# A two-layer block on one core: norm weights folded into a projection, one activation table set through attention, and gate steps moved into the expert stage

## The chip, the cores and the metric

The kernel runs on one core of a Trainium2 chip. The metric is the time of one execution in device microseconds (us). All data are float32. The core's engines are called as the profile calls them: PE is the matrix engine (PEld its weight loads), DVE the vector engine, ACT the scalar engine with its tables of functions, POOL the general engine, SP the engine whose queue issues most DMAs.

## The reference, cut to what matters

The input `x` is 4 rows (b = 0..3) of 512 tokens by 512 channels, `fside` has the same shape. Two layers follow each other; each part adds its result to `x`.

```python
def gate(r, k, v, w, u, time_emb):      # the four "cond" parts, l = 0..3; k = v = fside
    decay = f(w, time_emb)
    ek, ekv = exp(min(k, 30)), exp(min(k, 30)) * v
    # running sums over the tokens, forwards (nf, df) and backwards (nb, db): a = a * decay + e
    num = nf + nb - ekv + euk * v;  den = df + db - ek + euk     # euk = exp(min(u + k, 30))
    return sigmoid(r) * (num / max(den, 1e-8)) * (0.8 + 0.2 * tf)

x = x + mamba2(gate0(x))       # projection, short convolution, silu, a scan over the tokens in tiles;
                               # y = y * silu(z); y = y * rsqrt(mean(y*y) + eps) * norm_w; y @ out_proj_w.T
x = x + experts(gate1(x))      # top 2 of 8 experts per token, each a gated 512-512 network
x = x + attention(gate2(x))    # 16 heads in 4 groups with a shared key and value, causal softmax
x = x + ffn(gate3(x))          # silu(x @ gate) * (x @ up) @ down, 1408 wide
```

Everything of a gate but `sigmoid(r)` depends on `fside` alone, so it can be made before the row of `x` that it is for is ready.

## The kernel before

The program is unrolled, and written for a framework in which the code states instructions and tiles. A scheduler then orders the instructions of each engine by their place in the code, their data and the buffers of the tile pools, and sets the semaphores. `with after(engine)` holds a step behind the last instruction that the code has stated for that engine. Buffers with the same tag share `bufs` slots, so a tile waits until an older one is released. PSUM has three tags: `mm` (4 slots), `tp` (2 slots, `ps_tp`) and `acc` (2 slots).

Four stages follow each other:

- **Scan stage** (layer 0, `mamba2`; 16 tiles of 128 tokens, 4 per row). `start_tile` makes `z`, `start_scores`, `decays` and `outputs` make the tile's `y`. One half tile later, for the tile before it (`old`), `squares` and `norm` make the factor of the root mean square, `turn` transposes `y` into `pyt` (PSUM, tag `tp`) and writes it to `yT` times `norm_w` (first half: one DVE multiply, L1219; second half: four ACT multiplies, L1227), `project` multiplies it with `wot` (L1235), `scale` and `add_x` finish. `time_steps` and `sums` run once per row: `sums` (from L973) makes running sums over the tile's tokens with three products into `ppr` (tag `tp`), copies them to `cs` on DVE (L991), transposes `cs` on PE (`pcs`, L993), copies that to `csT` (L995) and stores it; `load_sums` reads it back, spread over the partitions.
- In the same stage the **gates** are made. `gate_pair` makes half a gate (2 of the 4 blocks of 128 channels): loads (`kt` L237, `ek` L244, `ekv` L246), four forward scans (L256) and four backward ones (L262) on DVE, sums (L273, L275, L277), then on ACT `Relu` (L313), `Ln` and `Exp` for the reciprocal, three more DVE steps (L319, L323, L328), and a store of `g` (L330). It is a generator: `pump(n)` runs n stretches of it, `nudge()` one short step. `gated` loads a made gate and applies it: four `Tanh` on ACT and four DVE steps (L383).
- `choose_experts` and `route` pick the experts of a row's tokens. They are a generator too (`routing`), stepped at fixed places of the tile loop.
- **Expert stage.** The tokens are sorted into 39 blocks of 128, one expert per block. `moe.round()` runs one block: first half (`pg` L775, `pn` L786), `finish` of the block before, `down` (`po` L808) of the block two before. Weights (`w1` in two halves of 1 MB, `w2` 1 MB) go out on SP's queue when a block's expert differs from the one that its buffer holds. The first 17 blocks use one set of buffers, the others two in turn. After each round but the last few, `more` runs `pump()` for the gates of layers l = 2 and 3.
- **Attention.** 16 groups of 4 heads, four (one per row) for each of the four key groups. Per head: `queries` (L1565), `scores` (psc L1582, mask L1585, maximum L1587, `Exp` on ACT L1592, L1594), then for the head before it `context` (L1605, L1608, L1614). After four heads `dense` (L1629). In each of a head's four score blocks `nudge()` runs a step of a gate. In the first groups `combine(b + 1)` adds the experts' results to the next row, and `gated(2, b + 1, ...)` gives that row's attention input; if its gate is not made yet, `gated` makes it there.
- **Feed-forward.** L1691, L1696, L1706 with `Silu` (L1700).

ACT holds one set of function tables at a time. `Tables` (the object `act`) loads a set by name (L112) and keeps the activations called through `act(...)` behind that load; the set stays until the next `act.use`. The set LOG_EXP has `Exp` and `Ln`, EXP has `Exp` and `Tanh`, SILU has `Silu` and `Tanh`. From `act.leave()` on (the last part of the scan stage's code) it keeps no record, and the compiler puts a load before every activation whose function is not in the set at hand.

Of the kernel before, what the change touches and what calls it, by code (L numbers as in the profile page):

```python
# [10 lines left out]
F32 = mybir.dt.float32  # L11
# [6 lines left out]
P = 128  # L18
# [62 lines left out]
def block_kernel(ctx: ExitStack, tc: tile.TileContext, a: dict, out: bass.AP):  # L81
# [424 lines left out]

    def route(lg, b, fine):
        n = NT * E
# [56 lines left out]
        yield  # L565
        pt = ps_tp("ptok")
        over = lambda v: v.unsqueeze(2).to_broadcast([P, NT, P])
        lanes = lane.unsqueeze(1).to_broadcast([P, NT, P])
        for c, (q, s_) in enumerate(vq):
            ov = tmp.tile([P, NT, P], F32, tag="th", name="ov")  # L570
            nc.vector.tensor_tensor(ov, lanes, over(q), ALU.is_equal)
            nc.vector.tensor_tensor(ov, ov, over(res_id[c][:, bt_]), ALU.mult)
            os_ = tmp.tile([P, NT, P], F32, tag="th", name="os")
            nc.vector.tensor_tensor(os_, lanes, over(s_), ALU.is_equal)
            for t in range(NT):
                nc.tensor.matmul(
                    pt[:, :P], lhsT=ov[:, t, :], rhs=os_[:, t, :],
                    start=(t == 0 and c == 0), stop=(t == NT - 1 and c == 1),
                )
# [15 lines left out]
    def choose_experts(b, xb, parts, pool, fine=False, **kw):  # L595

        lg = rt.tile([P, NT, E], F32, tag="lg", name="lg", bufs=2)
        nt = NT // parts
        for i in range(parts):
            h = gated(1, b, xb, pool, slice(i * nt * P, (i + 1) * nt * P), **kw)  # L600
            if fine:
                yield
            logits(h, b, lg, i * nt, nt)
            yield
        yield from route(lg, b, fine)

# [254 lines left out]
    with ExitStack() as ph:  # L861
# [64 lines left out]
        nc.sync.dma_start(out=wot, in_=a["out_projT"].rearrange("(k p) m -> p k m", p=P))  # L926

        def time_steps(w):

# [43 lines left out]
        def sums(w):  # L973
# [14 lines left out]
            nc.vector.tensor_tensor(dte, dt, ex[:, 1], ALU.mult)  # L988

            cs = sm.tile([P, n], F32, tag="cs", name="cs", bufs=2)  # L990
            nc.vector.tensor_copy(cs, pp[:, :n])  # L991
            pcs = ps_tp("pcs")
            nc.tensor.transpose(pcs[:n, :P], cs, ident)  # L993
            csT = four[:n, 0:2, :].rearrange("p i t -> p (i t)")
            nc.vector.tensor_copy(csT, pcs[:n, :P])  # L995
            nc.sync.dma_start(out=cs_d[w.b], in_=csT)
# [213 lines left out]
        def turn(u):  # L1210

            u.yT = sm.tile([P, NDI, P], F32, tag="yT", name="yT")
            for hh in range(2):
                pyt = ps_tp("pyt")
                for j in range(4):
                    js = slice(j * P, (j + 1) * P)
                    nc.tensor.transpose(pyt[:, js], u.y[hh][:, js], ident)
                if hh == 0:
                    nc.vector.tensor_tensor(  # L1219
                        u.yT[:, :4, :],  # L1220
                        pyt.rearrange("p (j t) -> p j t", t=P),
                        col("norm_w", 0, 4).unsqueeze(2).to_broadcast([P, 4, P]),
                        ALU.mult,
                    )
                else:
                    for j in range(4):
                        nc.scalar.mul(  # L1227
                            u.yT[:, 4 + j, :], pyt[:, j * P : (j + 1) * P], col("norm_w", 4 + j)
                        )

# [67 lines left out]
        for b in range(B):  # L1298
# [6 lines left out]
            for t in range(NT):  # L1305
# [86 lines left out]
                with after(*ENGINES):  # L1392
                    next(routing, None)
                    if b == B - 1 and t == 1:
                        next(routing)
# [75 lines left out]
    with tc.tile_pool(name="moe_w2", bufs=1, reuse_waits="tile") as wm:  # L1471
# [4 lines left out]
        def more(limit):  # L1476
            while moe.i < min(limit, moe.known):
                moe.round()
                if moe.i < NBLK - NT:
                    with after(nc.vector):  # L1480
                        pump()

# [28 lines left out]
    with att as ph:  # L1511
# [64 lines left out]
        def scores(u, i, qT):  # L1576

            prs = []
            for qi in range(NT):
# [11 lines left out]
                rsum = sm.tile([P, 1], F32, tag="rsum", name="rsum", bufs=4)  # L1591
                nc.scalar.activation(pr, psc[:, :n], AF.Exp, bias=nmax, accum_out=rsum)  # L1592
                nc.vector.reciprocal(rsum, rsum)
# [50 lines left out]
        def begin(n):  # L1644
# [5 lines left out]
            return groups[g, b], queries(groups[g, b], i)  # L1650

        groups = {}
        ready, held = begin(0), None
        for n, (g, b, i) in enumerate(heads_):
            u, qT = ready
            if g == 0 and i == 1 and b + 1 < B:
                combine(b + 1)
                hs[b + 1] = gated(2, b + 1, x[b + 1], gp, tag="h", name=f"h2_{b + 1}")
            if n + 1 < len(heads_):
                ready = begin(n + 1)  # L1660
            prs = scores(u, i, qT)
            if held is not None:
# [7 lines left out]
        for _ in making:  # L1670
            pass


    with ExitStack() as ph:
# [9 lines left out]
        for b in range(B):  # L1684
            h = gated(3, b, x[b], gp, tag="h", name=f"h3_{b}")
            hd = []
            for i in range(NFF):
# [11 lines left out]
                hi = sm.tile([P, T], F32, tag="hd", name="hd", bufs=NFF + 2)  # L1699
                nc.scalar.activation(hi, pg, AF.Silu, scale=col("gate_s", i))  # L1700
                nc.vector.scalar_tensor_tensor(hi, pu, col("up_s", i), hi, ALU.mult, ALU.mult)  # L1701
# [85 lines left out]
```

## Time and profile before

| | us |
|---|---|
| median of 3 runs (lowest, highest) | 2587.08 (2586.99, 2592.27) |
| the profiled execution | 2591.44 |
| its span in the trace | 2589.7 |
| PE busy in it | 2446.0 (94%) |
| DVE, ACT, POOL busy | 1409.8, 1032.3, 250.4 |

The profiled execution is 4.36 us longer than the median of the runs, and 1.74 us of it lie around the span. A row of the profile names a line of the code, an engine, an operation and the tiles (out<-in), then count, busy time in us and the mean of one in ns, and last the idle time of the engine ahead of it with the instruction that ended it. PEclk is the granted share of PE's clock.

By their chain of work the stages lie at about 0 to 665 us (scan, with a start of 80 us), 665 to 1165 us (experts), 1165 to 2128 us (attention) and 2128 to 2590 us (feed-forward).

### The profile page before, as it was taken

The numbers are of one execution on the slowest core, as the hardware profiler recorded it, in microseconds if no ns is written. First come the engines' busy times: TensorE is split into PE (matmuls) and PEld (weight loads), VectorE is DVE, ScalarE is ACT, GpSimd is POOL, SyncE is SP. The second block draws the span as 40 slices with busy tenths as digits, with TensorE's granted clock in tenths as the row PEclk, the third lists the DMA queues.
The fourth block names the chain that finished last, engine by engine and source line by source line (L and its number), as shares of the span: only waits on it lengthen the run. The fifth ranks groups of instructions, "written<-read, shape, count | busy, mean of one in ns | idle before, by whom it ended". The sixth has DMA issues, their size and how long they took to land.

```text
span 2589.7 us, 24584 instructions
## 1 busy us (share of the span) xinstructions
PE 2446.0 (94%) x8204; PEld 1301.0 (50%) x8204; DVE 1409.8 (54%) x2786; ACT 1032.3 (40%) x2129; POOL 250.4 (10%) x301
## 2 busy tenths in 40 slices
PE   3889998999999999999989999999999999999999
PEld 1555555556544444445545555555555554444444
DVE  8789998997335555646686554556544441010010
ACT  4666756657222333325554444344443431000000
POOL 1031323313211111120000000000000000000000
PEclk9979998999899999999999999999999999999999
DMA  6222523324244697745231101110000012000000
GB/s 217 77 94 76 188 69 112 131 80 159 66 175 140 223 337 283 274 177 163 75 92 46 46 27 29 45 45 30 21 25 17 17 69 82 17 0 16 8 8 16
DMA packets 88510, 244.09 MB, mean 94 GB/s; under 512 B 9536, under 2 KB 19136, under 8 KB 79296
## 3 DMA queue, kind: packets, MB, share of 16 engines
q1 hardware_dynamic: 79200, 215.78, 24.3%
q0 software_dynamic: 6880, 22.55, 2.5%
q10 hardware_dynamic: 2304, 4.20, 0.4%
q8 instruction: 65, 1.06, 0.2%
q14 instruction: 61, 0.50, 0.1%
HBM read 284.82 MB, written 47.05 MB: 128 GB/s over the span
## 4 chain that ended last, share of the span: by engine, by line
PE 75%; DVE 16%; ACT 4%; DMA 3%; issue 1%; POOL 0%; SPq 0%; ACTq 0%; DVEq 0%
PE pd L1629 8%; PE pq L1565 7%; PE pfu L1696 6%; PE pfo L1706 6%; PE pfg L1691 6%; PE pctx L1614 5%; PE po L808 5%; PE pg L775 5%; PE pn L786 5%; PE psc L1582 3%; PE pc L1007 2%; PE po L1235 2%; PE pv L1551 2%; PE ptp L1605 2%; PE pz L1078 2%; PE pk L1543 2%
## 5 line engine op out<-in xcount | busy, mean ns | idle before, releaser
L1565 PE MATMUL pq<-h,wq 128*128 128x512 f32 x512 | 248.0, 600 | 10.9 <-ACT pr L1592 10.9
L1629 PE MATMUL pd<-cx,wd 128*128 128x512 f32 x512 | 222.9, 593 | 1.3 <-DVE xr L1637 1.3
L1007 PE MATMUL pc<-h,wxb 128*128 128x512 f32 x320 | 151.6, 629 | 46.1 <-DVE h L1275 39.0
L1700 ACT ACTIVATE hd<-pfg,cols 128x512 f32<-128x512 f32 x44 | 30.3, 688 | 380.8 <-PE pfg L1691 380.8
L1701 DVE SCALAR_TENSOR_TENSOR hd<-pfu,cols,hd 128x512 f32<-128x512 f32 x44 | 33.0, 751 | 269.1 <-PE pfu L1696 269.0
L1585 DVE TENSOR_TENSOR psc<-psc,mask 128x128 f32<-128x128 f32 x256 | 72.2, 288 | 192.9 <-PE psc L1582 192.9
L1592 ACT ACTIVATE pr<-psc,nmax 128x128 f32<-128x128 f32 (+3 forms) x256 | 135.5, 530 | 95.6 <-DVE nmax L1587 94.9
L1614 PE MATMUL pctx<-pT,v 128*128 128x512 f32 (+3 forms) x512 | 153.6, 443 | 8.5 <-ACT pT L1608 5.1
L1696 PE MATMUL pfu<-h,ffu 128*128 128x512 f32 x352 | 158.7, 592 | 0.8 <-DMA ffu<-in_upT 0.8
L1691 PE MATMUL pfg<-h,ffg 128*128 128x512 f32 x352 | 158.6, 592 | 0.0
L1582 PE MATMUL psc<-kT,qT 128*128 128x128 f32 (+3 forms) x512 | 153.1, 439 | 3.1 <-ACT qT L1573 1.6
L1629 PEld LDWEIGHTS pd<-cx,wd 128*128 128x128 f32 x512 | 95.9, 190 | 116.8 <-issue 110.0
L1706 PE MATMUL pfo<-hd,ffd 128*128 128x512 f32 x352 | 151.7, 592 | 0.0
L775 PE MATMUL pg<-w,hT 128*128 128x512 f32 x312 | 144.7, 606 | 4.3 <-DMA w<-in_w1x 4.3
L1614 PEld LDWEIGHTS pctx<-pT,v 128*128 128x128 f32 x512 | 93.4, 190 | 99.6 <-issue 35.9
L808 PE MATMUL po<-w,yT 128*128 128x512 f32 x312 | 142.3, 596 | 1.2 <-DMA w<-in_w2x 1.2
L786 PE MATMUL pn<-w,hT 128*128 128x512 f32 x312 | 140.7, 592 | 0.0
L1637 DVE TENSOR_TENSOR xr<-xr,pd 128x512 f32<-128x512 f32 x64 | 44.0, 687 | 169.3 <-PE pd L1629 169.3
L1587 DVE TENSOR_REDUCE nmax<-psc 128x1 f32<-128x128 f32 (+3 forms) x256 | 124.0, 486 | 2.6
L1007 PEld LDWEIGHTS pc<-h,wxb 128*128 128x128 f32 x320 | 62.6, 201 | 119.6 <-issue 73.8
L1565 PEld LDWEIGHTS pq<-h,wq 128*128 128x128 f32 x512 | 87.1, 192 | 69.4 <-issue 56.1
L1605 PEld LDWEIGHTS ptp<-ident,pr 128*128 128x128 f32 x640 | 77.8, 142 | 87.4 <-issue 38.4
(308 smaller groups left out, 4220.2 us busy)
## 6 DMA issues: line engine op xcount, KB each, us to landing
w<-in_w1x SPq DMA_DIRECT2D x80, 1024.0 KB
w<-in_w2x SPq DMA_DIRECT2D x40, 1024.0 KB
wb<-in_b1x SPq DMA_DIRECT2D x40, 512.0 KB
lm<-cs SPq DMA_DIRECT2D x32, 512.0 KB
kt<-in_fT SPq DMA_DIRECT2D x62, 256.0 KB
ek<-ek SPq DMA_DIRECT2D x62, 256.0 KB
ekv<-ekv SPq DMA_DIRECT2D x62, 256.0 KB
g<-num SPq DMA_DIRECT2D x30, 512.0 KB
```

The lines of the kernel that those rows point to most:

```text
L775: nc.tensor.matmul(pg, lhsT=hT[:, k, :], rhs=self.w1[s][0][:, k, :], start=(k == 0), stop=(k == NC - 1))
L786: nc.tensor.matmul(pn, lhsT=hT[:, k, :], rhs=self.w1[s][1][:, k, :], start=(k == 0), stop=(k == NC - 1))
L808: nc.tensor.matmul(po, lhsT=yT[:, j, :], rhs=self.w2[s][:, j, :], start=(j == 0), stop=(j == NI - 1))
L1007: nc.tensor.matmul(pc, lhsT=wxb[:, k, m * P : (m + 1) * P], rhs=h[:, k, :], start=(k == 0), stop=(k == NC - 1),)
L1565: nc.tensor.matmul(pq, lhsT=u.wq[:, k, i * KVC : (i + 1) * KVC], rhs=u.h[:, k, :], start=(k == 0), stop=(k == NC - 1),)
L1582: nc.tensor.matmul(psc[:, :n], lhsT=qT[:, qi * P : n], rhs=u.kT[:, :n], start=True, stop=True)
L1592: nc.scalar.activation(pr, psc[:, :n], AF.Exp, bias=nmax, accum_out=rsum)
L1614: nc.tensor.matmul(pctx[:, kj * P :], lhsT=u.v[:, kj, :], rhs=pT[:, kj, kj * P :], start=(kj == 0), stop=(kj == NT - 1),)
L1629: nc.tensor.matmul(po, lhsT=u.wd[:, i, m * P : (m + 1) * P], rhs=u.ctxT[i], start=(i == 0), stop=(i == HPG - 1),)
L1691: nc.tensor.matmul(pg, lhsT=wg[:, k, cs], rhs=h[:, k, :], start=(k == 0), stop=(k == NC - 1))
L1696: nc.tensor.matmul(pu, lhsT=wu[:, k, cs], rhs=h[:, k, :], start=(k == 0), stop=(k == NC - 1))
L1706: nc.tensor.matmul(po, lhsT=wdn[:, i, m * P : (m + 1) * P], rhs=hd[i], start=(i == 0), stop=(i == NFF - 1),)
```

## The change

Five edits:

1. `norm_w` is multiplied into the rows of `wot` once, by 8 POOL instructions of 128x512, after its load. `turn` then only copies: two ACT copies of 128x512 per tile, and nothing on DVE.
2. In `sums` the transpose of `cs` is replaced by a fourth product into `ppr` that gives the turned sums at once (`dA` as the stationary side, `tri_le` moving); `pcs` is gone. `cs` is still copied.
3. In `route` for rows 0 to 2, the first pair of comparisons takes its own tile instead of the two `th` slots, a further `yield` stands after it, and the PSUM tile `ptok` is taken after the comparisons instead of ahead of them. In the last row `routing` is stepped once more.
4. In the expert stage `pump()` becomes `pump(1 + moe.i % 2)`: three stretches in two rounds.
5. In attention and feed-forward all activations go through `act`: LOG_EXP is held, EXP is loaded for each of three `gated` calls, and LOG_EXP again behind it; SILU is loaded at attention's end. `gated(2, b + 1, ...)` moves from the group's second head to its third, behind `begin(n + 1)`.

```diff
@@ route
+            if fine and c == 0:
+                both = pool.tile([P, 2, NT, P], F32, **kw)
+                ov, os_ = both[:, 0], both[:, 1]
+            else:
+                ov = tmp.tile([P, NT, P], F32, tag="th", name="ov")
+                os_ = tmp.tile([P, NT, P], F32, tag="th", name="os")
...
+            if fine and c == 0:
+                yield
+            if pt is None:
+                pt = ps_tp("ptok")
@@ scan stage, after the load of wot
+        for k in range(NDI):
+            nc.gpsimd.tensor_scalar(wot[:, k, :], wot[:, k, :], col("norm_w", k), None, ALU.mult)
@@ sums
+            nc.tensor.matmul(
+                pp[:n, 3 * n : 3 * n + P], lhsT=dA.rearrange("p t h -> p (t h)"), rhs=tri_le,
+                start=True, stop=True,
+            )
             cs = sm.tile([P, n], F32, tag="cs", name="cs", bufs=2)
             nc.vector.tensor_copy(cs, pp[:, :n])
-            pcs = ps_tp("pcs")
-            nc.tensor.transpose(pcs[:n, :P], cs, ident)
             csT = four[:n, 0:2, :].rearrange("p i t -> p (i t)")
-            nc.vector.tensor_copy(csT, pcs[:n, :P])
+            nc.vector.tensor_copy(csT, pp[:n, 3 * n : 3 * n + P])
@@ turn
-                if hh == 0:
-                    nc.vector.tensor_tensor(u.yT[:, :4, :], ...
-                else:
-                    for j in range(4):
-                        nc.scalar.mul(u.yT[:, 4 + j, :], ...
+                nc.scalar.copy(
+                    u.yT[:, hh * 4 : (hh + 1) * 4, :].rearrange("p j t -> p (j t)"), pyt
+                )
@@ tile loop
-                    if b == B - 1 and t == 1:
+                    if b == B - 1 and t < 2:
                         next(routing)
@@ more
-                        pump()
+                        pump(1 + moe.i % 2)
@@ scores
-                nc.scalar.activation(pr, psc[:, :n], AF.Exp, bias=nmax, accum_out=rsum)
+                act(pr, psc[:, :n], AF.Exp, bias=nmax, accum_out=rsum)
@@ attention's loop
+        with after(nc.scalar):
+            act.use(act.LOG_EXP)
...
             if g == 0 and i == 1 and b + 1 < B:
                 combine(b + 1)
-                hs[b + 1] = gated(2, b + 1, x[b + 1], gp, tag="h", name=f"h2_{b + 1}")
             if n + 1 < len(heads_):
                 ready = begin(n + 1)
+            if g == 0 and i == 2 and b + 1 < B:
+                act.use(act.EXP)
+                hs[b + 1] = gated(2, b + 1, x[b + 1], gp, tag="h", name=f"h2_{b + 1}")
+                act.use(act.LOG_EXP)
...
+        act.use(act.SILU)
@@ feed-forward
-                nc.scalar.activation(hi, pg, AF.Silu, scale=col("gate_s", i))
+                act(hi, pg, AF.Silu, scale=col("gate_s", i))
```

More of the change, by code (lines that the diff above doesn't have):

```diff
@@ L505, in logits, with route @@
             nc.sync.dma_start(out=rows_h[lo : lo + P, :], in_=hr)
-    def route(lg, b, fine):
+    def route(lg, b, fine, pool, **kw):
         n = NT * E
@@ L565, in route @@
         yield
-        pt = ps_tp("ptok")
         over = lambda v: v.unsqueeze(2).to_broadcast([P, NT, P])
         lanes = lane.unsqueeze(1).to_broadcast([P, NT, P])
+        pt = None
         for c, (q, s_) in enumerate(vq):
-            ov = tmp.tile([P, NT, P], F32, tag="th", name="ov")
+            if fine and c == 0:
[4 more added lines that the diff above has]
+                os_ = tmp.tile([P, NT, P], F32, tag="th", name="os")
             nc.vector.tensor_tensor(ov, lanes, over(q), ALU.is_equal)
             nc.vector.tensor_tensor(ov, ov, over(res_id[c][:, bt_]), ALU.mult)
-            os_ = tmp.tile([P, NT, P], F32, tag="th", name="os")
             nc.vector.tensor_tensor(os_, lanes, over(s_), ALU.is_equal)
+            if fine and c == 0:
+                yield
+            if pt is None:
+                pt = ps_tp("ptok")
             for t in range(NT):
@@ L604, in choose_experts @@
             yield
-        yield from route(lg, b, fine)
+        yield from route(lg, b, fine, pool, **kw)
     taken = rt.tile([P, 1], F32, name="taken")
@@ L1217, in turn @@
                     nc.tensor.transpose(pyt[:, js], u.y[hh][:, js], ident)
-                if hh == 0:
[L1219 to L1224, printed above, removed]
-                else:
-                    for j in range(4):
-                        nc.scalar.mul(
-                            u.yT[:, 4 + j, :], pyt[:, j * P : (j + 1) * P], col("norm_w", 4 + j)
-                        )
+                nc.scalar.copy(
+                    u.yT[:, hh * 4 : (hh + 1) * 4, :].rearrange("p j t -> p (j t)"), pyt
+                )
         def project(u):
```

## The prediction

> **What bounds the kernel now.** I read the page's slices first, then the engines' busy time by stage, who waited for whom on PE, and last single waits in the timeline.
>
> ```profile
> PE   3889998999999999999989999999999999999999
> DVE  8789998997335555646686554556544441010010
> ```
>
> PE is the bound nearly everywhere; DVE is about as full as PE in the scan stage (first ten slices) and half empty behind it. By stage (PE, PEld, DVE, ACT, POOL busy, granted clock, DMA share, GB/s):
>
> ```profile
> 80.00:665.00 585.00, 543.73 (x2249) 328.58 (x2249) 501.28 (x854) 386.57 (x766) 145.72 (x164) 0.94 0.33 109
> 665.00:1165.00 500.00, 482.50 (x1432) 239.06 (x1432) 249.30 (x402) 135.39 (x221) 94.68 (x107) 0.97 0.60 217
> 1165.00:1340.00 175.00, 157.84 (x578) 87.25 (x577) 125.73 (x276) 93.04 (x199) 1.11 (x1) 0.97 0.37 118
> 1340.00:2128.00 788.00, 767.52 (x2795) 427.00 (x2794) 414.58 (x1084) 350.33 (x848) 0.00 (x0) 1.00 0.10 32
> ```
>
> PE's own work hardly changes, so a gain can come only out of its idle time, 41, 18, 17 and 20 us in these stages, and out of the clock: 6% of 585 us is 35 us, 3% of 500 is 15, 3% of 175 is 5. The start (0 to 80 us, scans on DVE) and feed-forward (PE idle 6 us of 462, mostly its end) are untouched. PE's waits that the edits touch (us in total, times, longest):
>
> ```profile
> PE pq L1565 <- ACT pr L1592: 10.9, 5, 2.5
> PE pp L1094 <- DVE yT L1219: 7.9, 3, 4.8
> PE pg L775 <- DMA w<-in_w1x: 4.3, 2, 3.8
> PE pcs L993 <- DVE cs L991: 3.0, 3, 1.8
> ```
>
> The first is best seen in the timeline of ACT, then of PE:
>
> ```profile
> 1529.19 1.28 ACT L121 ACT_TABLE_LOAD   x1
> 1530.48 1.15 ACT L121 ACTIVATE rec<-rec,tiny 128x1024 f32<-128x1024 f32 x1
> 1531.65 1.28 ACT L1592 ACT_TABLE_LOAD   x1
> 1532.95 0.37 ACT L1592 ACTIVATE pr<-psc,nmax 128x128 f32<-128x128 f32 x1
> ```
> ```profile
> 1533.46 1.98 PE L1565 MATMUL pq<-h,wq 128*128 128x512 f32 x4 [2.50 <-ACT pr L1592]
> ```
>
> A gate's `Ln` needs another table set than the heads' `Exp`: load, `Ln`, load, 3.7 us in a row, and the head's first `Exp` stands behind; PE runs out of work for 2.50 us.
>
> **Part by part.** All sums are against the profiled execution (2591.44 us, span 2589.7), and are then taken from the median, 2587.08, which lies 4.36 lower.
>
> *Attention, one set (edit 5).* Behind 1340 us eight half gates end, each with such a pair of loads. Five times PE then waits: 2.50 (1533), 3.28 (1606), 2.48 (1693), 2.50 (1841), 2.66 us (1926). Without the loads the chain is 2 x 1.28 = 2.57 us shorter, so these 13.4 us go but for 0.7 at 1606; with the half clock that follows at 1607 (3.4 us at half rate, 1.7) I take **-15** (bounds -11 to -18). What is late next is DVE's queue, with the same gate steps as before.
>
> One rule of the Trainium skill differs here. The page "ScalarE: Activation LUTs", section "What ACT_TABLE_LOAD costs", adds a drain of 1380 ns to the load's 1283 ns for each switch. In this trace `Ln` starts 0.01 us behind the load, so no drain shows; by the page the pair would cost 5.3 us, but PE's measured waits would still cap the gain.
>
> *Attention's first groups (edits 4 and 5).* PE's chain shows where `dense` starts in each group:
>
> ```profile
> 1235.29 13.73 PE pd L1629 x32
> 1372.22 13.75 PE pd L1629 x32
> ...
> 1964.04 13.73 PE pd L1629 x32
> 2020.35 13.74 PE pd L1629 x32
> ```
>
> A group without gates takes 2020.35 - 1964.04 = 56.3 us. The two from 1235.29 to 1372.22 took 136.9, so 24.3 too much; 4.6 are `combine`'s 32 transposes (9.2 us for 64, L1460). Three half gates end in this stretch (1232, 1303, 1328 us), because `gated` forces them. One costs DVE about 18 us (4 scans of 1.22, 4 of 1.28, six steps of 0.70 to 0.72, three of 1.2 to 1.3). In the instruction order of the changed program all eight half gates of layer 2 stand in the expert stage (five before), and the eight of layer 3 are spread evenly, one in 1.3 groups. One of the three stays in effect; of 19.7 us excess I take two thirds: **-13** (-6 to -17).
>
> *The new loads* stand in the changed order as EXP, four `Tanh`, LOG_EXP, then the third head's `Exp`: three times 2.57 us of loads more on the chain that PE's next work hangs on, and the gate is now ready only one head ahead (about 9 us of PE: 56.3 less 13.7 for `dense` and 5.9 for key and value, over four) of its use instead of two. At the stage's start LOG_EXP and EXP both stand between the second and third `Tanh` of the first gate; ACT idles 1.35 us there today, so 1.2 of 2.57 us show. Hidden in full 0, all on the path 3 x 2.57 + 2.57 = 10.3; I take half, **+5**.
>
> *Expert stage (edit 4).* Three more half gates: 54 us of DVE, which has 250 idle, and six more loads on ACT, which has 365 idle. The price is on SP's queue: each stores its `g` there, and the next weights stand behind the store, which waits for DVE. In this stage's waits of SP's queue (total, times, longest), and in PE's timeline:
>
> ```profile
> SPq L330 <- DVE num L328: 49.3, 5, 12.6
> ```
> ```profile
> 871.02 1.19 PE L775 MATMUL pg<-w,hT 128*128 128x512 f32 x1 [3.75 <-DMA w<-in_w1x]
> ```
>
> The store at 863.5 was followed by this wait of 3.75 us, and by a clock of 0.66 in the next 10 us (3.4 us lost): 7.2 us. The one at 1040.0 led to 0.5 us; three cost nothing. So 7.7 us for five stores, 12.3 for eight: 4.6 more. A half gate moves 2 MB (six loads of 256 KB, a store of 512 KB), and the DMA engines are at 0.87 to 1.01 in most 10 us slices from 890 to 1020 us; in 890 to 1120 they have 40 us free, and two of the three half gates, which fall there, need 11 at the 359 GB/s of a full slice. **+6** (0: the waits only move; +22: half of the stores cost 7.2 us each).
>
> *Scan stage (edits 1 to 3).*
>
> ```profile
> L1219 DVE TENSOR_TENSOR yT<-pyt,cols 128x512 f32<-128x512 f32 x16 | 10.9, 681 | 3.1 <-PE pyt L1217 3.1
> L1227 ACT ACTIVATE yT<-pyt,cols 128x128 f32<-128x128 f32 x64 | 18.2, 365 | 13.2 <-PE pyt L1217 13.2
> L503 ACT COPY hr<-pht 128x512 f32<-128x512 f32 x16 | 9.1, 586 | 22.4 <-PE pht L499 22.2
> ```
>
> DVE loses 16 x 0.681 = 10.9 us; ACT gives 18.2 busy for 32 x 0.586 = 18.8. Three waits on DVE's half of `yT` (7.9 us, a `tp` slot not yet read) go with it, or turn into waits on ACT's queue. The fourth product replaces a transpose of the same 64x128 (0.27 us each); the copy to `cs` leaves PE's way (3.0 us), but the changed program makes the product wait for ACT's `Exp` of the same tile, which ended 0.45 us ahead of the first `pcs` and 1.7 us ahead of the second. `ptok` waited 4.7 us for comparisons. POOL's eight multiplies cost 0.6 us (as `skip` of 128x128) to 2.4 us (four times that) each, 5 to 19 us; POOL idles from 15 to 118.7 us and `wot` is first read at 142, so they cost nothing; without that cover, up to 19. The last row has one more load, 1.3 us of ACT, which is 66% busy. DVE's 10.9 count where DVE leads, about the half; with the named waits I take **-8** (-16: all of DVE's time and half of the rest; +4: ACT's queue holds `tp` for longer, at the last row's additional load above all).
>
> A rule speaks against this move: the same page, section "Rules for kernel authors", sends `add`, `mul` and the like to VectorE, not ScalarE. Here ACT's row for 128x512 from PSUM is the shorter (586 against 681 ns). By the rule the move would lose, by the rows it wins.
>
> **Sum:** -15 - 13 + 5 + 6 - 8 = -25: 2566 against the profiled run, **2562** against the median.
>
> **Rivals.**
>
> - *Slower: weights late in the expert stage.* Eight stores, and loads of `ekv` that wait for their only buffer with `w1` behind them in SP's queue; the DMA engines are full. For: the wait at 871, the slices near 1.0. Against: 0 us of PE idle from 950 to 1040 at the same fullness. If all eight cost 7.2 us that is 57.6, 50 more than now; with -31 elsewhere the kernel takes 2606. It decides from six of eight on (43.2 - 7.7 = 35.5 against 31).
> - *The waits change their name.* In attention DVE's gate steps or the table swaps ahead of the third heads hold PE instead, and the scan stage gives nothing: -15 - 3 + 10 + 6 = -2 to, with half of the 13, -9: about 2580. For: DVE is 72% busy from 1165 to 1340. Against: the groups without loads (56.3 us) show no such wait.
> - *More comes back.* All favourable ends: -18 - 17 + 0 - 16 + 1 = -50, 2537. For: the clock follows short gaps in the scan stage, 35 us lost there. Against: most of these gaps have other causes.
> - *An edit doesn't do what it says:* the turned sums trade a wait on DVE for one on ACT. Up to 3 us, inside the range.
>
> **How the numbers follow.** The forecast's case (2546 to 2576) has 0.58, "more" 0.13, "change their name" 0.15, "slower" 0.14. The range of 8 in 10 goes from the favourable ends, 2537, to 2592: the unfavourable ends together (-11 - 6 + 10 + 22 + 4 = +19, 2606) are left out, one or two of them are in. A difference of about 0.2% (5.2 us) is what can be told from none. Faster by more (below 2581.9): 0.58 + 0.13 + 0.07 = 0.78; within: 0.09; slower: 0.13.
>
> **What would show it.** In the changed profile: no load ahead of `Ln` behind 1165 us, and no PE wait of 2.5 us on `pr`; `dense` starts 58 to 62 us apart in the first groups; eight `g` stores before attention and at most three waits on `w1`; DVE about 11 us less busy in the scan stage, with no wait of `pp` on `yT` over 2 us. The prediction is wrong if the expert stage grows by over 20 us, or if attention does not shrink by at least 15.

## The result, and the profile after

| | us |
|---|---|
| before: median of 8 runs (lowest, highest) | 2587.03 (2582.49, 2592.27) |
| after: median of 8 runs (lowest, highest) | 2581.16 (2575.93, 2583.66) |
| after / before | 0.9977, 95% interval 0.9964 to 0.9989 |
| the profiled execution after, its span | 2578.31, 2576.6 |

The change saves 5.9 us where 25 were forecast. The two profiled executions lie 13.1 us apart, since the one before was above its median and the one after below its own. The stages tell more than the total. Each is read from the first product of a kind on PE (`pg`, then `pk`, then `pfg`), in us:

| stage | before | after | difference | forecast |
|---|---|---|---|---|
| scan, to the first `pg` | 678.0 | 663.7 | -14.3 | -8 |
| experts, to the first `pk` | 487.1 | 512.0 | +24.9 | +6 |
| attention, to the first `pfg` | 965.7 | 941.9 | -23.8 | -23 |
| feed-forward | 459.0 | 459.0 | 0 | 0 |

The scan stage's profiles differ by several us from one execution of the same code to the next: 672.3 to 678.0 in three kernels with the old code of it, 657.1 to 670.5 in eleven with the new. Their means, 674.6 and 664.2, make the gain 10. The expert stage is steady: ten kernels with the old number of gate steps show 484.4 to 487.7. So almost the whole miss lies there.

The slices of the page after:

```profile
PE   3879999999998899998999999999999999999999
DVE  8689999896345676746664655555434441010010
```

PE's eights in slices 13, 14 and 19 are the expert stage and its end. The expert stage by the windows view, before and after (PE, PEld, DVE, ACT, POOL busy, granted clock, DMA share, GB/s):

```profile
678.00:1165.10 487.10, 472.08 (x1386) 230.19 (x1386) 246.12 (x386) 132.57 (x213) 89.67 (x102) 0.98 0.61 220
663.70:1175.70 512.00, 479.13 (x1386) 230.35 (x1386) 291.12 (x433) 160.94 (x242) 91.83 (x102) 0.97 0.61 221
```

PE's idle time has grown by 17.9 us, from 15.0 to 32.9, and its same 1386 products take 7 us more; the mean granted clock is 0.97 instead of 0.98. DVE has 45 us more work, yet the DMA share is the 0.61 of before. What PE waited for in this stage, and below it what held SP's queue:

```profile
PE pg L783 <- DMA w<-in_w1x: 12.8, 6, 5.0
PE pg L783 <- ACT hT L756: 4.2, 1, 4.2
PE po L816 <- DMA w<-in_w2x: 3.6, 3, 1.8
PE po L816 <- ACT yT L809: 2.1, 4, 1.3
```
```profile
SPq L330 <- DVE num L328: 38.3, 7, 12.9
SPq L246 <- DVE num L256: 35.7, 9, 8.2
SPq L237 <- DVE eu L275: 23.7, 4, 11.9
```

Before, PE waited 5.5 us for weights and not at all for `hT`. Now it is 16.4 for weights and 6.3 for ACT's copies: together 17.2 us more, nearly all of the 17.9. SP's queue stood 97.7 us at transfers of the gates that wait for DVE; it was 76.8 before. Its stores of `g` (L330) have a smaller part in that than before, 38.3 us instead of 49.3; what has grown are the loads (L246 and L237), from 27.5 to 59.4.

In attention the waits on `pr` have lost their 2.5 us. These are all of `pq` and `pk` in the run, and the starts of `dense` in the first groups:

```profile
PE pk L1547 <- ACT pr L125: 2.6, 2, 2.1
PE pq L1569 <- ACT pr L125: 2.2, 2, 1.8
```
```profile
1248.46 13.73 PE pd L1633 x32
1314.21 13.73 PE pd L1633 x32
1379.01 13.73 PE pd L1633 x32
1435.50 13.74 PE pd L1633 x32
```

The intervals are 65.7, 64.9 and 56.5 us; the first two were 68.2 and 68.8. From the third `dense` to feed-forward attention takes 738.7 us, 20.0 less than before; its first part, from the first `pk` to there, 203.2, only 3.8 less.

### The profile page after: what moved, and what is told of

Its sections match the earlier page's. It is cut to its first block, busy times and chain, and to the rows that moved or that the text cites. A ratio compares the mean times of both kernels' runs of the same rounds, so it can differ in the third digit from the quotient of the medians.

```text
span 2576.6 us, 24557 instructions
## 1 busy us (share of the span) xinstructions
PE 2437.4 (95%) x8208; PEld 1297.3 (50%) x8208; DVE 1408.5 (55%) x2782; ACT 1014.4 (39%) x2078; POOL 282.5 (11%) x309
## 4 chain that ended last, share of the span: by engine, by line
PE 52%; DVE 4%; ACT 2%; DMA 1%; issue 0%; SPq 0%; ACTq 0%; DVEq 0%
PE pd L1633 8%; PE pq L1569 7%; PE pfu L1707 6%; PE pfo L1717 6%; PE pfg L1702 6%; PE pctx L1618 5%; PE psc L1586 3%; PE pv L1555 2%; PE pk L1547 2%; PE ptp L1609 2%; PE pg L783 1%; PE pn L794 1%; PE po L816 1%; DVE nmax L1591 1%; DVE psc L1589 0%; DVE num L256 0%
## 5 line engine op out<-in xcount | busy, mean ns | idle before, releaser
L783 PE MATMUL pg<-w,hT 128*128 128x512 f32 x312 | 150.6, 626 | 17.9 <-DMA w<-in_w1x 12.8
L1577 ACT ACTIVATE qT<-pq 128x512 f32<-128x512 f32 x64 | 38.2, 597 | 234.6 <-PE pq L1569 234.5
## 6 DMA issues: line engine op xcount, KB each, us to landing
wb<-in_b1x SPq DMA_DIRECT2D x40, 512.0 KB
lm<-cs SPq DMA_DIRECT2D x32, 512.0 KB
g<-num SPq DMA_DIRECT2D x30, 512.0 KB
```

Of the source, the lines that this page charges most:

```text
L783: nc.tensor.matmul(pg, lhsT=hT[:, k, :], rhs=self.w1[s][0][:, k, :], start=(k == 0), stop=(k == NC - 1))
```

## The experiments: the edits apart

Line numbers shift by a few between the kernels. "Before" is timed again on the same chip in each case.

**Edit 5 alone** (before, with LOG_EXP, EXP and SILU held as in the change).

> The kernel before with edit 5 alone (one table set through attention, the later gate application, the SILU load). By the prediction's step the attention stage, 965.7 us before from the first pk to the first pfg, loses the five waits of 2.5 us and a half of the early swaps' price: -15 to -10 us, the other stages stay within 3 us, total about 2575. Rival: the gain of 24 us seen in the changed kernel's attention comes from the moved gates, and the tables alone give under 5 us, since DVE's gate steps hold PE instead.

Measured: 2592.63 us, 1.0024 of before (1.0013 to 1.0035). From the third `dense` on attention fell by 15.9 us, the forecast's -15. But the second interval of `dense` became 91.5 us (68.8 before). ACT's timeline shows why, and then PE's:

```profile
1342.86 1.28 ACT L125 ACT_TABLE_LOAD   x1
1344.15 1.06 ACT L125 ACTIVATE rec<-rec 128x1024 f32<-128x1024 f32 x1
1358.46 1.23 ACT L125 ACTIVATE th<-xr 128x512 f32<-128x512 f32 x2 [13.25 <-DVE h L383]
1359.71 1.28 ACT L112 ACT_TABLE_LOAD   x1
1361.01 0.37 ACT L125 ACTIVATE pr<-psc,nmax 128x128 f32<-128x128 f32 x1
```
```profile
1361.52 6.31 PE L1543 MATMUL pk<-h,wkv 128*128 128x512 f32 x8 [21.76 <-ACT pr L125]
```

`gated` stands between the loads of EXP and LOG_EXP. When its half gate is not yet made, it makes it right there: ACT idles 13.25 us in that stretch, and the heads' `Exp` (`pr`) may come only behind LOG_EXP at 1359.71. PE then stands still for 21.76 us. The edit saves in the steady part and pays it back at one place.

**Edit 4 alone** (`pump(1 + moe.i % 2)`).

> The kernel before with edit 4 alone (three stretches of gates in two rounds of blocks). Theory: this edit by itself makes the expert stage longer, by about 25 us (487 us from the first pg to the first pk before, 512 in the changed kernel), and the attention shorter by 8 to 13, so the total is 10 to 17 us over the kernel before, about 2600. Rival: the expert stage's loss is the scan stage's gain given back (weights and rows that are not there yet when the stage starts 14 us earlier); then this kernel's expert stage stays within 5 us of 487 and the total is 2575 to 2580.

Measured: 2608.75 us, 1.0079 (1.006 to 1.0098). The expert stage takes 520.0 us, 32.9 more; attention 956.6, 9.1 less. Alone this edit loses. With eight half gates the expert stage is less steady than with five: 520.0 us here, 512.0 in the full change.

**Edits 1 to 3 alone.**

> The kernel before with edits 1 to 3 alone (norm weights in the projection, turned sums by a product, the route's additional step). Theory: the expert stage starts 14 us earlier, as in the changed kernel (664 against 678 us), in spite of a start that is 4 us later, and expert stage and attention stay as before: total about 2573. Rival, as above: what is won in the scan stage is lost in the expert stage, total 2585 to 2590.

Measured: 2575.61 us, 0.9957 (0.9944 to 0.9971). Its median lies 5.6 us below the full change's, though the intervals of the two ratios overlap. The other stages are as before (486.3, 965.4, 459.0).

**All but edit 4.**

> The changed kernel with edit 4 undone, one stretch in each round. Theory: the expert stage is back at 487 us or up to 5 more, the scan stage keeps its 14 us, the attention keeps the tables' part, 10 to 15 us: total 2560 to 2568, which is what the prediction had for the whole change. Rival: without edit 4 the first groups of attention are bound by DVE and by the forced gates, with table loads for each, so that attention gains under 8 us and the total is not below 2575.

Measured: 2585.93 us, 0.9999 (0.9984 to 1.0013). The expert stage is back at 486.9, and the second interval is 91.1 again. So in the full change edit 4 costs 25 us in one stage and takes away the forced gate that would cost about 23 in the next (attention's first part is 230.5 us without edit 4, 207.0 before).

**The missing half gate made ahead of the load of EXP**, in place of edit 4:

```diff
-                        pump(1 + moe.i % 2)
+                        pump()
...
                 combine(b + 1)
+                have((2, b + 1))
```

> Edits 1, 2, 3 and 5 without edit 4, and one call added: behind combine(b + 1), ahead of the load of EXP, the missing half gate is made to its end. That run without the added call had its second interval of dense at 91.1 us, first part of attention 230.5, expert stage 486.9, whole span 2580.9. Theory (the heads' Exp stood behind the forced gate because LOG_EXP was loaded only behind it): the second interval falls to 66 to 69 us, the first part of attention to 205 to 210, the span to 2555 to 2560 and the median to about 2562, under both kernels. Rival (the forced gate costs PE its DVE and SP time, not the table): the interval stays above 80 us and the median at 2580 or more.

Measured: 2563.37 us, 0.9916 (0.9897 to 0.9935). The second interval is 72.1, attention's first part 211.1, the expert stage 484.4. The gate is still forced, but ACT keeps its tables while that happens. So 19 of the 22 us by which the second interval had grown go with the order around the loads; interval and first part stay a little above what was expected. The call also makes the gate one head earlier than `gated` did, and that part was not tried apart.

## The experiments: the expert stage

Three explanations stood for the 25 us: weights held in SP's queue behind the gates' transfers; DMA engines that are full; and the order on ACT (and DVE), where the round's copies stand behind the gate's own steps. The changed kernel's timeline shows the first and the third within 30 us of each other. ACT, then PE, then SP's queue:

```profile
806.35 1.28 ACT L121 ACT_TABLE_LOAD   x1
807.64 1.15 ACT L121 ACTIVATE rec<-rec,tiny 128x1024 f32<-128x1024 f32 x1
808.81 1.28 ACT L121 ACT_TABLE_LOAD   x1
810.10 1.06 ACT L121 ACTIVATE rec<-rec 128x1024 f32<-128x1024 f32 x1
811.07 0.58 ACT L809 ACTIVATE yT<-pyt 128x512 f32<-128x512 f32 x1
811.54 0.58 ACT L756 COPY hT<-pfl 128x512 f32<-128x512 f32 x1
```
```profile
812.17 6.25 PE L783 MATMUL pg<-w,hT 128*128 128x512 f32 x8 [4.18 <-ACT hT L756]
...
842.30 4.60 PE L783 MATMUL pg<-w,hT 128*128 128x512 f32 x5 [4.96 <-DMA w<-in_w1x]
```
```profile
826.92 0.07 SPq L721 DMA_DIRECT2D wb<-in_b1x  x1
834.58 0.34 SPq L330 DMA_DIRECT2D g<-num  x1
835.33 0.34 SPq L716 DMA_DIRECT2D w<-in_w1x  x1
```

At 812 `hT` came 4.18 us late, behind load, `Ln`, load and `Exp` of a gate; and the eight products then took 6.25 us instead of 3.60, at a granted clock of 0.59. From 827.0 SP's queue issued nothing for 7.6 us, until the store of `g` could go at 834.58; the weights followed 0.75 us later, and `pg` waited 4.96 us for them.

The Trainium skill says the same of the wait's place (page "DMA: Bandwidth & Descriptors", section "Anatomy of one DMA — SWDGE (gpsimd) path", in a sentence on DMA engines at large): the DMA engines do not wait on semaphores, the issuing sequencer does so before it hands a transfer out. The gap from 826.92 to 834.58 in SP's queue agrees.

**The store of g one stretch later** (layer 2 only; a list of stores that the next `pump`, `nudge` or `gated` issues):

> The changed kernel with all five edits; for the gates of layer 2 alone the store of g is stated one stretch of the generator later (or with the next nudge, or ahead of the load in gated), so that in SP's queue it stands about half a round behind the steps that it waits for. Everything else as in the changed kernel, whose expert stage takes 512.0 us against 487.1 before. Theory 1 (the queue: w1, w2 and b1 go out behind a store of g that waits for DVE, and reach PE late): the stage falls to 490 to 502 us, the waits of pg on w1 from 12.8 us to under 7, the whole to about 2565 to 2572. Theory 2 (the DMA engines are full, and the 6 MB of three more half gates push the weights back): the stage stays at 508 to 515, the same weights are late. Theory 3 (order on ACT and DVE: hT and g stand behind the gates' own steps): 508 to 515 too, with waits of pg on hT and of b1 on DVE unchanged.

Measured: 2576.46 us, 0.9961 (0.9945 to 0.9977); expert stage 512.7. SP's waits at stores fell from 38.3 to 27.7 us, but at the long wait the store still stood ahead of the weights (835.91 and 836.66): a stretch later is often the same round. The run moved too little to decide.

**No Ln in layer 2's gates** (`Relu` in its place).

> The changed kernel, but the gates of layer 2 have Relu in the place of Ln: the two table loads around Ln are gone, the step itself stays; the values of these gates are other than the reference's. Theory 3 (ACT's chain load, Ln, load, Exp of about 5 us holds the round's hT and then g): the expert stage falls from 512.0 by eight half gates of 1.5 to 2.6 us, to 492 to 500. Theories 1 and 2 (queue, DMA engines): the stores come at most 2.6 us earlier, the stage stays at 505 to 512.

Measured: expert stage 508.7, 3.3 less, total 2571.95 in one run. The wait on `hT` fell to 1.6, but PE's waits on weights rose from 16.4 to 21.4.

**More traffic, first form** (a 256 KB copy per round).

> Edits 1 to 3 alone (expert stage 486.3 us), and with each round of the expert stage that runs gate steps one copy of 256 KB from DRAM to DRAM on POOL's queue, that waits for nothing but the copy two before: some 27 times 512 KB read and written, over twice the 6 MB that edit 4 moves into the stage, on the same DMA engines, but without a place in SP's queue and without work on DVE or ACT. Theory 2 (the DMA engines are full): the stage grows by 15 us or more, to over 500, with more waits of pg and po on weights. Theories 1 and 3: it grows by 0 to 7 us.

Nothing held these copies in place, and all were issued between 15 and 102 us; the expert stage (484.0) says nothing. They hit the start instead: the first `pz` came at 94.5 us, against 88.1 without them.

**More traffic, second form:**

```diff
+                    with after(nc.gpsimd):
+                        nc.gpsimd.dma_start(out=spare[moe.i % 2], in_=a["fT"][:P, 0, :])
```

> Edits 1 to 3 alone (expert stage 486.3 us) with one copy of 256 KB from DRAM to DRAM on POOL's queue in each round of the expert stage that runs gate steps, now put in POOL's order behind the round's gather and scatter, since the copies without that place had all been issued in the first 102 us. About 7 MB more in the stage, against 6 MB of the three half gates that edit 4 moves in. Theory 2 (the DMA engines are full): the stage grows by 12 us or more, to 498 to 512, with more waits of pg and po on weights. Theories 1 and 3: it grows by 0 to 6 us.

Measured: 29 copies between 760 and 1091 us, expert stage 488.2, 1.9 more; 235 GB/s instead of 221, a DMA share of 0.66 instead of 0.61. More bytes than the three half gates bring do not make the 25 us, so full DMA engines are out as their main cause.

**The gates' transfers on POOL's queue** (layer 2):

```diff
-            nc.sync.dma_start(out=kt[i], ...
+            queue = nc.gpsimd if l == 2 else nc.sync
+            queue.dma_start(out=kt[i], ...     # ek, ekv and the store of g likewise
```

> The changed kernel; for the gates of layer 2 alone the loads of kt, ek and ekv and the store of g go out on POOL's queue instead of SP's, so that w1, w2 and their biases never stand behind a gate's transfer that waits for DVE. The transfers, the DVE and the ACT steps are the same. Expert stage of the changed kernel 512.0 us, 487.1 before. Theory 1 (head of SP's queue held by loads and stores of the gates, 97.7 us of waits on DVE there): the stage falls to 485 to 498 us, the waits of pg on w1 from 12.8 us to under 5. Theory 2 (DMA engines full): 506 to 515. Theory 3 (order on ACT and DVE): 505 to 512, hT at about 812 still 4 us late. POOL's queue also gathers the blocks' rows three rounds ahead; if a waiting store holds these, pfl waits on hb appear and the stage does not fall, which tells nothing of theory 1.

Measured: 2574.36 us, 0.9951 (0.9931 to 0.9971); expert stage 506.3, 5.7 less. The wait at 842 is gone. PE's waits:

```profile
PE pg L785 <- ACT hT L758: 7.4, 4, 4.8
PE po L818 <- ACT yT L811: 4.5, 2, 4.2
PE pg L785 <- DMA w<-in_w1x: 3.3, 2, 1.8
PE po L818 <- DMA w<-in_w2x: 3.0, 2, 2.4
```

The weights come in time (`pg` on w1 3.3 us instead of 12.8), and PE waits for ACT instead: 11.9 us on `hT` and `yT`, 6.3 before that.

**Only the loads on POOL's queue.**

> As the run before, but only the loads of kt, ek and ekv of layer 2's gates go out on POOL's queue; the store of g stays on SP's. Under theory 1 it shows which of the two holds the weights: if the loads do (59.4 us of waits for DVE in SP's queue), the stage falls nearly as far, to 488 to 500; if the stores do (38.3 us), it stays at 505 to 512. Theories 2 and 3: 505 to 515.

Measured: 518.3. The stores' waits in SP's queue rose from 38.3 to 72.5 us, and PE waited 15.1 us for weights. So with the loads gone from the queue, the stores alone hold it for 72.5 us, where loads and stores together held it for 97.7. PE's waits for ACT's copies rose as well, from 6.3 to 11.5 us, and the stage became 6.3 us longer.

**Both: POOL's queue and no Ln.**

> The changed kernel with both edits for the gates of layer 2: all their transfers on POOL's queue, and Relu in the place of Ln (so these gates' values are not the reference's). Expert stage: 512.0 in the changed kernel, 506.3 with the queue alone, 508.7 without Ln alone, 487.1 before. If the queue and ACT's chain of loads are two causes that stand in for each other (with one gone PE waits for the other), the stage falls by more than the 9.0 us that the two gave singly, to 490 to 500 us. If they are independent and something else holds the rest, it is 501 to 505.

Measured: 493.6, total 2559.2 in one run. Singly the two gave 5.7 and 3.3 us; together they give 18.4. What is left of PE's waits for weights and ACT's copies:

```profile
PE pg L788 <- ACT hT L761: 4.1, 2, 2.1
PE po L821 <- DMA w<-in_w2x: 2.4, 1, 2.4
PE pn L799 <- DMA w<-in_w1x: 1.6, 2, 1.3
PE po L821 <- ACT yT L814: 0.5, 2, 0.3
```

| PE's waits, us | weights | `hT`, `yT` | expert stage |
|---|---|---|---|
| before | 5.5 | 0 | 487.1 |
| after | 16.4 | 6.3 | 512.0 |
| no Ln | 21.4 | 2.1 | 508.7 |
| POOL's queue | 7.7 | 11.9 | 506.3 |
| only the loads on it | 15.1 | 11.5 | 518.3 |
| both | 4.0 | 4.6 | 493.6 |

Taken singly, each cure lets the other wait grow. 18.4 of the 24.9 us come back with both, as two causes that cover for each other; of the last 6.5 the runs don't tell the cause. Two things limit this. Both runs without `Ln` are single ones. And the cures were not tried on five half gates: with both, PE waits 4.0 us for weights, less than the 5.5 of before, so a small part of the 18.4 may not belong to the three added gates.

**No gate steps at all in the stage.**

> Edits 1 to 3 alone with no step of a gate in the expert stage: the gates of layers 2 and 3 are all made in attention, which becomes much longer and is not read here; only the expert stage is, which was 486.3 us with five half gates and 512.0 with eight. If every half gate costs PE about the same (8.3 us, as the three of edit 4), the stage falls to about 445 to 455 us, which PE's own work of 472 us forbids; so the price must grow with their number. If the first five fit beside the experts' work, the stage stays at 476 to 486.

Measured: from the first `pg` to the last `po` 475.9 us, PE idle 7.8 of them. (The stage as a whole shows 535.0, because row 0's gate is then made at its end, with PE waiting.) By the same marks it is 486.6 with five half gates and 511.6 with eight. The first five cost 2.1 us each, the next three 8.3. Edit 4 changes the pace as well as the number, since every other round now runs two stretches; no run has eight half gates at one stretch a round, so which of the two makes the later ones dear is open.

## The experiments: the scan stage

**Edit 1 alone.**

> The kernel before with edit 1 alone (norm_w into wot on POOL; turn as two ACT copies). Scan stage 678.0 before, 664.8 with edits 1 to 3. The prediction gave the three edits -8 together, most of it from DVE's 10.9 us in this one. If edit 1 carries the gain, in spite of 3 us lost at the start to POOL beside DVE: 666 to 671, the whole at 0.9965 to 0.998 of before. If the sums or the routing carry it: 676 to 682.

Measured: 1.0012 (0.9997 to 1.0027), scan stage 676.0. No gain. The first `pz` comes at 89.5 us, 4.4 later than before, and from there to the first `pg` it takes 586.5 us, against 587.1 to 592.9 in the three kernels with the old code: what edit 1 may win behind the start is too little to tell. DVE's busy time there fell from 502.8 to 494.7 us.

**Edit 2 alone.**

> The kernel before with edit 2 alone (turned sums by a fourth product; no transpose behind the copy to cs). Priced in the prediction at 0 to -3 us, as the wait on DVE's cs (3.0 us in three) gives way to one on ACT's Exp. Expected: scan stage 675 to 679, the whole at 0.9985 to 1.0005 of before. If the sums carry the scan stage's gain: 668 to 672.

Measured: 1.0019 (1.001 to 1.0029), scan stage 675.0. A small loss.

**Edit 3 alone.**

> The kernel before with edit 3 alone (the first comparisons of a row's routing in their own tile with a yield behind them, ptok taken after them, one more step of the routing in the last row). The prediction counted it only as the 4.7 us of ptok's waits. If it carries the gain of edits 1 to 3 (0.9957): scan stage 664 to 668, the whole at 0.995 to 0.997 of before. If it gives only its waits: 0.9975 to 0.999. If the three work only together: 0.999 to 1.001.

Measured: 2577.23 us, 0.9966 (0.9954 to 0.9977), scan stage 659.4. The windows of before and of this run, in the same 200 us:

```profile
300.00:500.00 200.00, 188.89 (x791) 115.34 (x790) 178.59 (x304) 128.96 (x251) 52.03 (x53) 0.93 0.35 118
```
```profile
300.00:500.00 200.00, 193.73 (x834) 117.60 (x833) 184.16 (x319) 137.39 (x268) 54.54 (x59) 0.97 0.35 119
```

PE gets 43 more products done. Before, this stretch had, among others, gaps of 1.36 us (`ptok` on the comparisons at 399.8), 4.78 (`pp` on `yT` at 429.8) and 1.99; now the longest is 2.11, and the clock is 0.97 instead of 0.93. The edit states the comparisons a step ahead of the products that read them and takes `ptok` after them, so a `tp` slot is held for less time; that this slot, and not the extra step, is the cause is argued, not shown.

**Edits 1 and 3.**

> The kernel before with edits 1 and 3, without the turned sums. If the routing's order needs the DVE time that edit 1 frees, or carries the gain alone: 0.995 to 0.997 of before, as edits 1 to 3 together. If the turned sums are needed too: 0.998 to 1.001.

Measured: 0.9988 (0.9974 to 1.0003), scan stage 673.0: a smaller gain than edit 3 alone, though the intervals overlap a little. With edit 2 as well it is 0.9957. Edit 3 carries the gain, edit 1 seems to take some of it back, and edit 2, a small loss alone, helps beside edits 1 and 3. Why it does was not tried apart: by the waits, `pcs` on DVE's `cs` is 6.3 us with edits 1 and 3, and 2.9 (`ppr` on ACT's `ex`) with all three.

**The multiplies of wot on ACT instead of POOL**, on top of the missing half gate made first:

```diff
-            nc.gpsimd.tensor_scalar(wot[:, k, :], wot[:, k, :], col("norm_w", k), None, ALU.mult)
...
+        with after(nc.scalar):
+            for k in range(NDI):
+                nc.scalar.mul(wot[:, k, :], wot[:, k, :], col("norm_w", k))
         pump(4)
```

> Edits 1, 2, 3, 5 and the missing half gate made ahead of the load of EXP (2563 us median, span 2553.7), with the eight multiplies of wot by norm_w on ACT, which idles from 42 to 49 us, instead of POOL. Theory (POOL's multiplies, 21 us from 40 us on, slow DVE's steps beside them by up to a third, and all of the start hangs on DVE): no DVE step from 44 to 56 us takes longer than in the kernel before, the first pz comes at 85 to 87 us instead of 89.8, the span falls by 2 to 4 us to about 2550. Rival (the delay is from the change in order of xc and pdt, not from POOL): the first pz stays at 88 to 90.

Measured: 2558.51 us, 0.9898 (0.9879 to 0.9917), the best of all; 0.9916 (0.9897 to 0.9935) with the multiplies on POOL, so the intervals overlap and the last 5 us are not certain. The start is earlier beyond doubt: the first `pz` comes at 84.2 us, against 89.8 there, 89.3 in the changed kernel and 85.1 before. DVE's steps of the changed kernel, beside POOL's multiplies, and then of this run:

```profile
51.89 1.57 DVE L256 TENSOR_TENSOR_SCAN den<-decay,ek 128x512 f32<-128x512 f32 x1
53.38 1.64 DVE L262 TENSOR_TENSOR_SCAN num<-decay,num,f 128x511 f32<-128x511 f32 x1
54.95 1.11 DVE L251 TENSOR_TENSOR ekv<-ek,kt 128x512 f32<-128x512 f32 x1
```
```profile
51.73 1.20 DVE L256 TENSOR_TENSOR_SCAN den<-decay,ek 128x512 f32<-128x512 f32 x1
52.85 1.26 DVE L262 TENSOR_TENSOR_SCAN num<-decay,num,f 128x511 f32<-128x511 f32 x1
54.02 0.67 DVE L251 TENSOR_TENSOR ekv<-ek,kt 128x512 f32<-128x512 f32 x1
```

The groups of the multiplies, on POOL in the changed kernel and on ACT in this one (count, ns shortest/median/longest):

```profile
L937 POOL TENSOR_SCALAR wot<-wot,cols x8: 1580/2060/6248, 39.9 to 58.7; 128x512 f32<-128x512 f32 x8
```
```profile
L1283 ACT ACTIVATE wot<-wot,cols x8: 705/706/707, 41.5 to 45.8; 128x512 f32<-128x512 f32 x8
```

DVE's longer steps are only the first part of the delay. PE's next products in the kernel before, then in the changed one:

```profile
78.07 3.72 PE L934 MATMUL pdt<-wxb,h 128*128 128x16 f32 x32 [0.26 <-DVE xc L1022]
```
```profile
79.45 6.42 PE L945 MATMUL pdt<-wxb,h 128*128 128x16 f32 x32 [2.70 <-DVE xc L1035]
```

`pdt` starts 1.4 us later, behind a gap of 2.70 us instead of 0.26. Then its 32 products take 2.7 us more: the granted clock is 0.50 from 80.1 to 90.3 us, where before it was 0.50 only from 81.7 to 85.1. So most of the 4.2 us at the first `pz` is the slower clock behind that gap.

## Why the prediction was right or wrong

- **Expert stage, +6: the step that failed.** It measured +24.9. The step said "The price is on SP's queue" and took 7.7 us for five stores, so 12.3 for eight. The five half gates cost about 11 us and the next three 25: the price of one is not a constant. What the runs showed in its place are two waits that cover for each other: 10.9 us more for weights behind SP's queue, and 6.3 us for ACT's copies, which the step did not have. Our reading, not tried by a run of its own, is that a late transfer or copy is absorbed while there is slack in SP's prefetch and on ACT, and that the added ones meet it used up. The step also priced six more loads on ACT at nothing, "365 idle": at 806 to 811 they stood in front of `hT`, on the path. That idle share is of the whole stage, and says nothing of the 5 us in which a copy is due. And since the two causes cover for each other, a sum of single prices could not find them.
- **Its rival.** "Weights late in the expert stage" named the queue and reached +50. That mechanism was there, at a third of its price: 16.4 us of waits on weights for eight stores, where it had 57.6. The bounds of +22 for the term were too narrow by 3 us.
- **Attention, one set, -15.** Right, mechanism and size: 15.9 for edit 5 alone in the steady part, 20.0 with edit 4, no `Ln` waits left.
- **First groups, -13, and new loads, +5.** Together -8, measured -3.8. The two intervals stayed at 65.7 and 64.9 us, not 58 to 62. The excess was misread: in the 136.9 us before, PE was busy for 124.4, where two intervals of 56.3 without gates are 112.6. So 11.8 of the 24.3 us were PE's own work or its slower clock, not 4.6, and only 12.5 were idle. The change brought the idle time to 6.6 and left the busy time at 124.0. That edits 4 and 5 need each other was missed too: without edit 4 the loads around a forced gate cost 23 us there. The prediction saw "the gate is now ready only one head ahead", but priced only the loads' own 2.57 us, not the gate that may be made between them.
- **Scan stage, -8.** -10 by the means, inside its bounds, for the wrong reason and so by luck. Most of the term was DVE's 10.9 us of edit 1, which alone gave nothing that can be told; `ptok`'s "4.7 us for comparisons" was a side remark, and edit 3 is what gained 10 us.
- **Start "untouched", POOL's multiplies at 0.** Wrong: 4.2 us later at the first `pz`. The named cover, POOL's idle time, was there, but the multiplies took 21.0 us, over the 5 to 19 that they were given. Some of DVE's steps beside them became up to two thirds longer, DVE is the start's bound, and behind the gap ahead of `pdt` PE's clock was at a half for three times as long.
- **What should show it.** Eight stores of `g` in the stage, no load ahead of `Ln` in attention, no wait of 2.5 us on `pr`: so it was. DVE "about 11 us less busy in the scan stage": 502.8 to 491.8 us from the first `pz` to the first `pg`, as foreseen, though the gain came from elsewhere. "At most three waits on `w1`": six. No wait of `pp` on `yT` over 2 us: three on ACT's copy, 4.5 us in all, the longest 2.6. The prediction's own mark for being wrong, an expert stage longer by over 20 us, was met.

In the sum of favourable ends the expert stage stands with +1 where its own bound is 0, which moves that end by 1 us.

With the expert stage at its +6 the change would have come within a few us of the forecast; the other errors nearly cancel, which is luck.

## What to carry to other kernels

In this kernel the sixth to eighth unit of background work cost four times what the first five did. So look at the slack that is left at the place where such work goes, and not only at what a unit of it cost before: two steps that each had cover can lose it together, and an experiment that removes one cause shows little until the other is removed too. Before a function table is swapped around a call, make everything that the call might make on demand. And an idle engine was not free here where it worked beside the engine that sets the pace.

## What the hardware showed unexpectedly

POOL's 128x512 multiplies in SBUF slowed some of DVE's steps beside them: from 1.20 to 1.57 us for a scan, from 0.67 to 1.11 for a product of two tiles. At other times POOL was the one that waited: its first multiply took 6.25 us, from 39.85 to 46.10, while DVE's steps up to 44.8 kept their time, and where its multiplies took 1.6 to 2.0 us DVE's were the longer ones. ACT's eight took 0.71 us each, and DVE's steps beside them took 1.21 to 1.27 us, as before. The Trainium skill has a reason (page "GPSIMD Engine Reference", section "1. Specifications"): GpSimd shares its SBUF interfaces with VectorE, with contention for VectorE instructions in a 2-port perf mode or with two SBUF inputs. The slowed steps shown have two such inputs, so rows and page agree in that. The prediction had not drawn on it.
